# Loads of x on GpSimd's queue in a cross-attention kernel

## Chip, cores and metric

The kernel runs on one core of a Trainium2 chip. A time is the device time of one execution in microseconds (us), and the time before is the median of three executions. TensorE, VectorE, ScalarE, GpSimd and SyncE are the core's engines; in the profile they are PE (with PEld, its weight loads), DVE, ACT, POOL and SP.

## What is computed

The reference is a cross-attention over 32 batches of 512 rows of x, 640 wide, with 20 heads of 32, a context of 77 keys, an output projection with a bias, and the input x added at the end. The context holds only 77 tokens, so the slices for objects, others and images in the reference are empty and add nothing. In float32:

```python
residual = hidden_states
q = _heads(hidden_states @ to_q_w)
h_txt = _sdpa(q, _heads(ehs_txt @ to_k_w), _heads(ehs_txt @ to_v_w))
...
out = _merge(h_txt) + SCALE_OBJ * _merge(h_obj) + SCALE_OTH * _merge(h_oth) + SCALE_IP * _merge(h_ip)
out = out @ to_out_w + to_out_b
out = (out + residual) / RESCALE
```

## The kernel before

**Precision.** Each matrix product is done as three products of split numbers (a high part and a rest, `PAIRS`), so a projection of 640 channels takes 15 matmuls for 512 columns.

**Phases.** Up to about 285 us the kernel computes keys and values of all batches and stores them in device memory (`k_dram`, `v_dram`). After that runs a pipeline of N = 160 slots: slot n treats batch b = n // 5 and a group of four heads j = n % 5. `slot(n)` writes out the order of work of every engine by hand (`manual_schedule`): each engine, SyncE with its DMA issues too, does its instructions in program order, and waits at each for what it needs.

**A slot.** Per slot there are four score tiles of 128 rows (`scores`), the exponentials on ScalarE (`exps`), and the following work of other heads:

- `queries(n + 1, ...)`: the next slot's q, on TensorE (L332), and `split_q`, which splits it on ScalarE and VectorE (L343 to L349).
- `normalize(n - 1, ...)`: GpSimd multiplies the last slot's exponentials by the reciprocal sums (L400).
- `transpose_p(n - 1)`: VectorE transposes them into the tile `z` (L407), and four DMAs write z to device memory (`pd`, L414). z has one buffer, so the next transpose waits until these four have read it. `load_p` reads them back in the wanted order (`raw`, L423 and L424), some slots later.
- `cast_p`, `rest_p`, `last_p`: the split of the loaded p on ScalarE (L431, L437), VectorE (L438) and GpSimd (L445), into `pp`.
- `values`: TensorE multiplies pp and the values (L459), eight passes; the last two use the part that `last_p` writes.
- `piece`: TensorE's output projection (L489); `finish` adds it to a row block of the residual `xr` on VectorE (L517) and stores it (L521). `load_residual` loads that block (L478), and `add_bias` adds the bias to it on GpSimd (L482), before.
- `refill`: parts of the keys and values of this or the next batch (L309, L312, L319).

**x.** `load_x(b)` loads a whole batch of x into the tile `xs` with four DMAs of 320 KB, one for each 32 partitions; each consists of 32 x 16 runs of 160 floats. The tile has one buffer. `transpose_x` turns it in four pieces on VectorE (L272), one in slot 0, two in slot 1 and one in slot 2 of the batch ahead of its use; `split_x` splits it into `xt`, five blocks on ScalarE (L279) and GpSimd (L280), in slots 2 and 3. In slot 4 of batch b the tile is free and `load_x(b + 2)` fills it. The loads for batches 0 and 1 are issued ahead of the pipeline.

**Order in the middle of slot 4.** After the second score tile come `load_p`, `refill` (nothing in slot 4), `finish`, `load_x`, `load_residual`, and `add_bias`. GpSimd's work in a slot comes in the order `normalize`, `last_p`, `add_bias` and, in slots 2 and 3, `split_x`. All DMAs of the kernel are issued by SyncE.

Of the kernel before, what the change touches and what calls it, by code (L numbers as in the profile page):

```python
# [24 lines left out]
Q = 32  # L25
# [25 lines left out]
def kernel(  # L51
# [25 lines left out]
    nc = tc.nc  # L77
# [181 lines left out]

    xts, raws, pps, ats, xss, pds, sms, pqs, pas, xrs, pos = ({} for _ in range(11))  # L260

    def load_x(b):

        xs = main.tile([P, S // Q, C // 4], F32, tag="xs", name="xs")
        src = x[b].rearrange("(a j) (q u) -> q j a u", j=Q, q=4)
        for q in range(4):
            nc.sync.dma_start(xs[q * Q : (q + 1) * Q, :, :], src[q])
        xss[b] = xs

    def transpose_x(b, i):  # L270
# [82 lines left out]
    def scores(n, t):  # L353
        b, j = divmod(n, NC_)
        g = GROUP_OF[j]
        qt, (kb, kc) = qts[n % 2], kbs[g]
        jg = j - GROUPS[g][0]
        sc = ps.tile([P, S], F32, tag="sc", name="sc", bufs=3)
        half = KCOLS // 2
        for m, (cols, keys_) in enumerate(  # L360
            (
                (slice(0, KCOLS), kb[:, jg]),
                (slice(0, half), kc[:, jg, 0]),
                (slice(half, KCOLS), kc[:, jg, 1]),
            )
        ):
            nc.tensor.matmul(  # L367
                sc[:, cols],
                qt[:, m, t * P : (t + 1) * P],
                keys_,  # L370
                start=(m == 0),
                stop=(m == 2),
            )
        nm = main.tile([P, HPC], F32, tag="nm", name="nm", bufs=3)
        nc.vector.tensor_reduce(  # L375
            nm, sc[:, :KCOLS].rearrange("p (h k) -> p h k", k=NKEY), AX.X, ALU.max, negate=True
        )
        return sc, nm
# [14 lines left out]
    def sums(n):  # L393
        rs = main.tile([P, NQ * HPC], F32, tag="rs", name="rs", bufs=2)
        nc.vector.reciprocal(rs, sms.pop(n))  # L395
        return rs

    def normalize(n, rs):
        pf = pnb[n % 2][:, :, :NKEY]
        nc.gpsimd.tensor_tensor(  # L400
            pf, pf, rs.unsqueeze(2).to_broadcast([P, NQ * HPC, NKEY]), ALU.mult
        )
# [17 lines left out]
    def load_p(n):  # L420
        pd = pds.pop(n)
        raw = late[0].tile([P, 3, S], F32, tag="raw", name="raw", bufs=2)
        nc.sync.dma_start(raw[:, 0:2, :], pd[0 : 2 * P, :].rearrange("(k p) q -> p k q", p=P))  # L423
        nc.sync.dma_start(raw[:64, 2, :], pd[2 * P :, :])  # L424
        raws[n] = raw

    def cast_p(n):

        raw = raws[n]
        pp = late[0].tile([P, 5, S], FPR, tag="pp", name="pp", bufs=1)  # L430
        nc.scalar.copy(pp[:, 0:2, :], raw[:, 0:2, :])  # L431
        pps[n] = pp

    def rest_p(n):

        raw, pp = raws[n], pps[n]
        nc.scalar.copy(pp[:64, 4, :], raw[:64, 2, :])  # L437
        nc.vector.tensor_tensor(  # L438
            pp[:, 2:4, :], raw[:, 0:2, :], pp[:, 0:2, :].bitcast(F32), ALU.subtract
        )  # L440

    def last_p(n):

        raw, pp = raws.pop(n), pps[n]
        nc.gpsimd.tensor_tensor(  # L445
            pp[64:, 4, :], raw[:64, 2, :], pp[:64, 4, :].bitcast(F32), ALU.subtract
        )
# [27 lines left out]
    def load_residual(b, t, xr=None):  # L475
        if xr is None:
            xr = late[0].tile([P, C], F32, tag="xr", name="xr", bufs=3)
        nc.sync.dma_start(xr, x[b, t * P : (t + 1) * P, :])  # L478
        xrs[b, t] = xr
# [31 lines left out]
    def finish():  # L511

        while closed:
            b, t, h = closed.pop(0)
            xr = xrs[b, t]
            cols = slice(h * HALF, (h + 1) * HALF)
            nc.vector.tensor_tensor(  # L517
                xr[:, cols], pos.pop((b, t, h))[:, :HALF], xr[:, cols], ALU.add
            )
            if h == 1:  # L520
                nc.sync.dma_start(out[b, t * P : (t + 1) * P, :], xr)  # L521
# [11 lines left out]
    RESIDUAL = {1: (1, 0), 2: (1, 1), 3: (1, 2), 4: (1, 3)}  # L533
# [9 lines left out]
    def refill(b, j, part):  # L543

        heads = range(2 * part, 2 * part + 2)
        segments = SEGMENTS[4 * part : 4 * part + 4]
        if j == 0:
            load_keys(b, 1, heads)
        elif j == 1:
            load_values(b, 0, segments)  # L550
        elif j == 2 and b + 1 < B:
            load_keys(b + 1, 0, heads)
        elif j == 3:
            load_values(b, 1, segments)

    def slot(n, beside=None):
        b, j = divmod(n, NC_)
        ahead, more = n + 1 < N, b + 1 < B
        back, first = PIECES[j]
        bo_, has_out = b - back, b >= back  # L560
        xsplits = SPLIT_X.get(j, ((), ())) if more else ((), ())
        turns = TRANSPOSE_X.get(j, ((), (), ())) if more else ((), (), ())
        taken, second = takes.get(n), seconds.get(n)

        refill(b, j, 0)
        if taken is not None:
            cast_p(taken)
        s = scores(n, 0)
        if taken is not None:
            rest_p(taken)  # L570
        if n:
            normalize(n - 1, sums(n - 1))
        if taken is not None:
            last_p(taken)
        exps(n, 0, *s)
        if ahead:
            queries(n + 1, 0, 2)
        s = scores(n, 1)
        if n - LAG + 1 in pds and n > LATE:
            load_p(n - LAG + 1)  # L580
        refill(b, j, 1)
        finish()
        if j == 4 and b + 2 < B:
            load_x(b + 2)
        if j in RESIDUAL and b >= RESIDUAL[j][0]:
            load_residual(b - RESIDUAL[j][0], RESIDUAL[j][1])
        if j in BIAS and b >= BIAS[j][0]:
            add_bias(b - BIAS[j][0], BIAS[j][1])
        exps(n, 1, *s)
        for i in turns[0]:  # L590
            transpose_x(b + 1, i)
        if ahead:
            queries(n + 1, 2, NC_)
        s = scores(n, 2)
        if n:
            transpose_p(n - 1)
        if ahead:
            split_q(n + 1)
        exps(n, 2, *s)
        for c in xsplits[0]:  # L600
            split_x(b + 1, c)
        if has_out:
            piece(bo_, first)
        if taken is not None:
            values(taken)
        if beside:
            beside()
        s = scores(n, 3)
        finish()
        for i in turns[1]:  # L610
            transpose_x(b + 1, i)
        if taken is not None:
            split_a(taken)
        for c in xsplits[1]:
            split_x(b + 1, c)
        exps(n, 3, *s)
        if has_out:
            piece(bo_, first + 1)
        for i in turns[2]:
            transpose_x(b + 1, i)  # L620
        if second is not None:
            cast_p(second)
            rest_p(second)
            last_p(second)
            take(second)
            if second + 2 in pds and second + 2 not in takes.values():
                load_p(second + 2)
# [66 lines left out]

    with tc.manual_schedule(engines=ENGINES):
        g0, gn = GROUPS_KV[-1]
        load_x(0)
        load_keys(0, 0)
        for h in range(2):
            context_values(g0, gn, 0, h, psv)  # L700
        for i in range(NQ):
            transpose_x(0, i)
        for c in range(NC_):
            split_x(0, c, nc.gpsimd if c % 2 else nc.vector)
        load_x(1)
        for t0 in (P, 2 * P):
            for h in range(2):
                context_values(g0, gn, t0, h, psv)
        queries(0, 0, NC_)
        split_q(0)  # L710
        for n in range(LATE):
            slot(n, (lambda: context_values(g0, gn, 3 * P, n // 2, psv)) if n % 2 else None)
        psv.release()
        kvp.release()
        late.append(ctx.enter_context(tc.tile_pool(name="late", bufs=1, reuse_waits="tile")))
        late.append(
            ctx.enter_context(tc.tile_pool(name="psl", bufs=1, space=PSUM, reuse_waits="tile"))
        )
        load_p(0)
        load_p(1)  # L720
        wos.append(late[0].tile([P, NC_, 2, C], FPR, name="wo_s"))
        for n in range(LATE, LATE + 4):
            slot(n)
            for k in {LATE: (0, 1), LATE + 1: (2, 3), LATE + 2: (4,)}.get(n, ()):
                nc.sync.dma_start(wos[0][:, k].bitcast(F32), wo_dram[:, k].bitcast(F32))
        for n in range(LATE + 4, N):
            slot(n)
        end()
# [40 lines left out]
```

## Time and profile before

| What | Value |
|---|---|
| Median of 3 runs | 2026.93 us (2025.39 to 2027.08) |
| Profiled execution | 2018.67 us, span 2016.9 us |
| Mean granted TensorE clock | 0.989 |
| Busy, VectorE / ScalarE / GpSimd | 1354.7 / 1588.0 / 981.9 us |
| Loads of x: issues, time of one issue, issue to landing | 128, 0.487 us, 7.5 us (medians) |
| Writes of p: issues, time of one issue, issue to landing | 640, 0.520 us, 3.6 us (medians) |

The profile is of one execution, and all its times are from the start of the span. A row of a timeline has the start, the time taken, the engine, the line, the operation, what is written from what, and in brackets the idle time of the engine before it with what ended that. A row of waits reads: who waited for whom, microseconds in total, times, the longest.

### The profile page before, as it was taken

What the parts mean: (1) busy time and instruction counts of PE and PEld (TensorE: products, weight loads), DVE (VectorE), ACT (ScalarE), POOL (GpSimd) and SP (SyncE); (2) the same over time, 40 slices, a digit from 0 to 9 for tenths busy, and PEclk for the clock granted to TensorE, in tenths of its full rate; (3) what the DMA queues carried; (4) which work ended last, traced back from release to release, by engine and by line L of the source; (5) the groups of instructions that cost most, each with busy time, mean ns of one, the idle gap of its engine ahead of it and who ended that gap; (6) DMA issues with size and microseconds to landing.
All of it is one profiled execution on the core that took longest, in us unless ns stands there. A gap on an engine that the chain in (4) does not pass through costs nothing.

```text
span 2016.9 us, 38271 instructions
## 1 busy us (share of the span) xinstructions
PE 1963.4 (97%) x11012; PEld 1763.5 (87%) x11012; DVE 1354.7 (67%) x2159; ACT 1588.0 (79%) x6377; POOL 981.9 (49%) x617
## 2 busy tenths in 40 slices
PE   9999997899999999999999999999999999999998
PEld 7889986789888988888898888888888888988898
DVE  4443225777777777777777677777777777777764
ACT  3321128889889988888898899899898889989993
POOL 0000023555555555555556555666555655555554
PEclk9999998999999999999999999999999999999999
DMA  7993366888888888888988888888888888888875
GB/s 172 221 255 108 105 148 151 222 222 221 223 223 220 226 218 226 217 218 218 229 226 220 208 227 229 222 223 218 217 222 219 218 224 218 228 222 222 222 202 169
DMA packets 555997, 423.55 MB, mean 210 GB/s; under 512 B 170191, under 2 KB 459501, under 8 KB 555789
## 3 DMA queue, kind: packets, MB, share of 16 engines
q1 hardware_dynamic: 555789, 421.10, 82.4%
q8 instruction: 91, 1.49, 0.3%
q14 instruction: 117, 0.96, 0.1%
HBM read 245.61 MB, written 175.32 MB: 209 GB/s over the span
## 4 chain that ended last, share of the span: by engine, by line
PE 54%; DMA 19%; SPq 8%; POOL 6%; issue 5%; ACT 4%; DVE 4%; DVEq 0%; POOLq 0%; ACTq 0%
PE pq L332 17%; PE po L489 15%; DMA pd<-z 8%; PE pa L459 8%; PE sc L367 6%; POOL pn L400 4%; PE pv L197 4%; PE pk L168 4%; DMA xs<-in_x_dram 3%; DMA raw<-pd 3%; SPq L414 2%; DVE qt L349 2%; ACT pn L385 2%; POOL pp L445 2%; DMA kb<-k_dram 1%
## 5 line engine op out<-in xcount | busy, mean ns | idle before, releaser
L385 ACT ACTIVATE pn<-sc,nm 128x77 f32<-128x77 f32 x2560 | 799.2, 329 | 109.3 <-DVE nm L375 96.5
L400 POOL TENSOR_TENSOR pn<-pn,rs 128x1232 f32<-128x1232 f32 x160 | 364.5, 2278 | 692.6 <-DVE rs L395 541.2
L489 PE MATMUL po<-wo_s,at 128*128 128x320 f32 x3840 | 627.6, 313 | 1.4 <-DVE xr L517 1.4
L332 PE MATMUL pq<-xt,wq_s 128*128 128x512 f32 x2400 | 622.5, 400 | 0.0
L489 PEld LDWEIGHTS po<-wo_s,at 128*128 128x128 f32 x3840 | 567.0, 189 | 2.0 <-DVE xr L517 1.7
L385 ACT ACTIVATION_READ_ACCUMULATOR pn<-sc,nm 128x1 f32 x2560 | 530.6, 207 | 0.0
L332 PEld LDWEIGHTS pq<-xt,wq_s 128*128 128x128 f32 x2400 | 429.7, 190 | 77.5 <-POOL xt L280 0.2
L375 DVE TENSOR_REDUCE nm<-sc 128x4 f32<-128x308 f32 x640 | 294.0, 460 | 264.3 <-PE sc L367 258.1
L459 PE MATMUL pa<-pp,vb 128*128 128x512 f32 x1280 | 337.7, 402 | 19.6 <-ACT pp L431 9.9
L407 DVE STREAM_TRANSPOSE z<-pn 128x1280 f32<-128x1280 f32 x160 | 241.8, 1511 | 119.2 <-DMA pd<-z 62.4
L459 PEld LDWEIGHTS pa<-pp,vb 128*128 128x128 f32 x1280 | 242.5, 197 | 68.3 <-POOL pp L445 20.7
L367 PEld LDWEIGHTS sc<-kc,qt 128*128 128x128 f32 x1280 | 213.3, 189 | 40.9 <-issue 13.9
L367 PE MATMUL sc<-kc,qt 128*128 128x154 f32 x1280 | 227.1, 256 | 13.6 <-DVE qt L349 12.9
L438 DVE TENSOR_TENSOR pp<-raw,pp 128x1024 fp32r<-128x1024 f32 x160 | 196.2, 1226 | 50.1 <-ACT pp L431 34.3
L445 POOL TENSOR_TENSOR pp<-raw,pp 64x512 fp32r<-64x512 f32 x160 | 209.4, 1309 | 36.4 <-ACT pp L437 24.3
L349 DVE TENSOR_TENSOR qt<-pq,qt 64x512 fp32r<-64x512 f32 x320 | 214.3, 670 | 7.5 <-ACT qt L343 3.1
L280 POOL TENSOR_TENSOR xt<-xs,xt 128x512 fp32r<-128x512 f32 x157 | 199.7, 1299 | 16.8 <-ACT xt L279 12.2
L482 POOL TENSOR_TENSOR xr<-xr,bias 128x640 f32<-128x640 f32 x128 | 201.2, 1573 | 12.0 <-POOL pp L445 2.7
L347 ACT CAST qt<-qt 64x512 fp32r<-64x512 f32 x320 | 198.1, 619 | 9.0
L367 PE MATMUL sc<-kb,qt 128*128 128x308 f32 x640 | 196.0, 306 | 1.2 <-ACT qt L343 1.2
L431 ACT CAST pp<-raw 128x1024 fp32r<-128x1024 f32 x160 | 170.1, 1063 | 1.3 <-DVE at L105 0.8
L104 ACT CAST at<-pa 128x512 fp32r<-128x512 f32 x160 | 94.9, 593 | 75.5 <-PE pa L459 72.8
(41 smaller groups left out, 1536.3 us busy)
## 6 DMA issues: line engine op xcount, KB each, us to landing
pd<-z SPq DMA_DIRECT2D x640, 160.0 KB, 3.6
raw<-pd SPq DMA_DIRECT2D x160, 512.0 KB, 4.1
xs<-in_x_dram SPq DMA_DIRECT2D x128, 320.0 KB, 7.5
xr<-in_x_dram SPq DMA_DIRECT2D x128, 320.0 KB, 3.8
out_dram<-xr SPq DMA_DIRECT2D x128, 320.0 KB, 3.3
raw<-pd SPq DMA_DIRECT2D x160, 128.0 KB, 4.2
v_dram<-vs SPq DMA_DIRECT2D x19, 640.0 KB, 4.0
k_dram<-ks SPq DMA_DIRECT2D x80, 128.0 KB, 2.4
```

Of the source, the lines that this page charges most:

```text
L280: engine.tensor_tensor(parts[1], src, parts[0].bitcast(F32), ALU.subtract)
L332: nc.tensor.matmul(pqs[n], wq_s[:, k, a, j * P : (j + 1) * P], xts[b, k][:, c, :], start=(k == 0 and m == 0), stop=(k == NC_ - 1 and m == 2),)
L349: nc.vector.tensor_tensor(qt[r, 1 + w, :], pq[r], qt[r, 0, :].bitcast(F32), ALU.subtract)
L367: nc.tensor.matmul(sc[:, cols], qt[:, m, t * P : (t + 1) * P], keys_, start=(m == 0), stop=(m == 2),)
L375: nc.vector.tensor_reduce(nm, sc[:, :KCOLS].rearrange("p (h k) -> p h k", k=NKEY), AX.X, ALU.max, negate=True)
L385: nc.scalar.activation(pnb[n % 2][:, at, :NKEY], sc[:, i * NKEY : (i + 1) * NKEY], AF.Exp, bias=nm[:, i : i + 1], accum_out=sms[n][:, at : ...
L400: nc.gpsimd.tensor_tensor(pf, pf, rs.unsqueeze(2).to_broadcast([P, NQ * HPC, NKEY]), ALU.mult)
L407: nc.vector.transpose(z.rearrange("p b t j -> p t b j"), pn.rearrange("p (t h) k -> p t (h k)", t=NQ).rearrange("p t (b i) -> p t b i", i=Q),)
L445: nc.gpsimd.tensor_tensor(pp[64:, 4, :], raw[:64, 2, :], pp[:64, 4, :].bitcast(F32), ALU.subtract)
L459: nc.tensor.matmul(pas[n], vb[:, t, :, a], pp[:, c, :], start=(m == 0), stop=(m == len(PASSES) - 1),)
L482: nc.gpsimd.tensor_tensor(xrs[b, t], xrs[b, t], bias, ALU.add)
L489: nc.tensor.matmul(pos[b, t, h][:, :HALF], ats[b * NC_ + j][:, a, t * P : (t + 1) * P], wos[0][:, j, c, h * HALF : (h + 1) * HALF], start= ...
```

## The change

`load_x` takes the issuing engine as an argument, GpSimd if none is named. The two loads ahead of the pipeline stay on SyncE; those in slot 4, 30 of them with four DMAs each, are issued by GpSimd, at its place in program order between `last_p` and `add_bias` of that slot. In the program `load_residual` now stands ahead of `load_x`. Shapes, buffers and all arithmetic stay.

```diff
-    def load_x(b):
+    def load_x(b, engine=nc.gpsimd):
...
-            nc.sync.dma_start(xs[q * Q : (q + 1) * Q, :, :], src[q])
+            engine.dma_start(xs[q * Q : (q + 1) * Q, :, :], src[q])
...
+        if j in RESIDUAL and b >= RESIDUAL[j][0]:
+            load_residual(b - RESIDUAL[j][0], RESIDUAL[j][1])
         if j == 4 and b + 2 < B:
             load_x(b + 2)
-        if j in RESIDUAL and b >= RESIDUAL[j][0]:
-            load_residual(b - RESIDUAL[j][0], RESIDUAL[j][1])
...
-        load_x(0)
+        load_x(0, nc.sync)
...
-        load_x(1)
+        load_x(1, nc.sync)
```

## The prediction

> **What bounds the kernel now.** I read the page's engine shares first, then the waits of each engine over the steady stretch (380 to 1925 us), then the timelines of all engines over one batch.
>
> ```profile
> span 2016.9 us, 38271 instructions
> PE 1963.4 (97%) x11012; PEld 1763.5 (87%) x11012; DVE 1354.7 (67%) x2159; ACT 1588.0 (79%) x6377; POOL 981.9 (49%) x617
> ...
> q1 hardware_dynamic: 555789, 421.10, 82.4%
> ```
>
> TensorE sets the pace: 97% busy, granted clock 1.00 in the steady windows, and one slot after another starts its projection of queries at 962.26, 972.59 and 982.90 us, so a slot that nothing disturbs takes 10.32 us and a batch of five 51.6. All DMAs are in one hardware queue, and GpSimd issues none. What can still be won is what TensorE waits for. Its waits in the steady stretch, and VectorE's beside them:
>
> ```profile
> PE sc L367 <- DVE qt L349: 9.0, 24, 0.8
> PE pa L459 <- POOL pp L445: 6.4, 24, 0.8
> ...
> DVE z L407 <- DMA pd<-z: 62.4, 23, 4.0
> ```
>
> Both TensorE waits come about once per batch, as the wait of the transpose of p for the writes of the former p (z has one buffer) does. The timeline of VectorE shows where: a batch's first slot, right behind the load of x.
>
> ```profile
> 987.30 0.48 DVE L375 TENSOR_REDUCE nm<-sc 128x4 f32<-128x308 f32 x1 [1.78 <-PE sc L367]
> 990.59 1.51 DVE L407 STREAM_TRANSPOSE z<-pn 128x1280 f32<-128x1280 f32 x1 [2.81 <-DMA pd<-z]
> 992.02 1.37 DVE L349 TENSOR_TENSOR qt<-pq,qt 64x512 fp32r<-64x512 f32 x2
> 993.42 0.48 DVE L375 TENSOR_REDUCE nm<-sc 128x4 f32<-128x308 f32 x1
> ...
> 994.34 0.83 DVE L272 STREAM_TRANSPOSE xs<-xs 128x640 f32<-128x640 f32 x1
> ```
>
> And the timeline of SyncE shows why: four loads of x (4 x 320 KB) enter the queue ahead of the writes of p.
>
> ```profile
> 976.65 1.95 SPq L267 DMA_DIRECT2D xs<-in_x_dram  x4
> 978.64 1.21 SPq L478 DMA_DIRECT2D xr<-in_x_dram  x1
> 979.90 3.50 SPq L414 DMA_DIRECT2D pd<-z  x4
> ```
>
> Those four writes land 8.2 to 9.5 us after issue; the kernel's median for such a write is 3.6, and the four issued from 969.44 also took 3.6. The last lands when z is given free, at 990.5, while GpSimd had its normalized p ready at 987.61. The split of q starts late, TensorE waits 0.27 us for it, and a slot later 0.23 for GpSimd's pp, which the same delay pushed back. The whole price is read from the starts of the normalizations: from 420.41 to 1891.63 us, 28 batches took 52.54 us each. The steps into slots 2, 3, 4 and 0 are the same in all, about 9.53, 10.12, 10.50 and 9.98; only the step from slot 0 to slot 1 varies, between 11.38 and 14.24. Against 51.6 this is 0.94 us a batch, 28 us for the 30 batches that load an x this way. The waits that the view books make only 15.4; the rest lies in matmuls drawn longer than their spacing.
>
> **The change, part by part.**
> Removed from SyncE: 120 of the 128 loads of x, four in each of 30 batches, 4 x 0.487 = 1.95 us a batch. SyncE isn't the bound, and by itself this only lets the residual load and the writes of p go out earlier; the writes wait for the transpose, which ends at 979.17, so they gain some 0.7 us.
>
> The residual's load, now ahead in the program, is on another engine than the load of x, and its order against SyncE's other work is otherwise kept: nothing.
>
> Taken out of the queue ahead of p: 1.31 MB. The stretch from 979 to 984 us moves 200 GB/s and that from 982.6 to 993 moves 229, so 1.31 MB is 5.7 to 6.6 us of all engines; the writes of p are late by 8.9 - 3.6 = 5.3. If x goes beside them in a queue of its own, with half the engines' time at worst, 0.66 MB of p takes 6 us and is read out by about 986, before the 987.61 at which it is wanted. The wait of VectorE goes, and with it up to 28 us. On the same 16 engines the sum of the bytes stays, so x gives up what p gains, and x is what is late next. At half of 220 GB/s its 1.31 MB takes 11.9 us from about 980, so it lands near 992. It is wanted by the first transpose of x: 994.34 in this batch, about 991.5 without VectorE's 2.81 us stall. VectorE can be some 2.5 us late there before TensorE waits (that is 2.81 less the 0.27 that came through). So a wait of half a microsecond lies in that cover, and is costed at nothing; without cover it is 0.5 x 30 = 15 us.
>
> Added on GpSimd: four DMA issues per batch, between the pp of slot 4 and the bias add of that slot. Their own wait, for the readers of xs, is long over (the last split of x ends at 973.96). Queued behind them are the bias add (1.57 us; its rows are finished only in the next batch's first slot), then the normalization of slot 0, and behind that the pp of slot 0, for which TensorE's value matmuls wait.
>
> ```profile
> 977.71 1.29 POOL L445 TENSOR_TENSOR pp<-raw,pp 64x512 fp32r<-64x512 f32 x1
> 979.08 1.57 POOL L482 TENSOR_TENSOR xr<-xr,bias 128x640 f32<-128x640 f32 x1
> 985.33 2.28 POOL L400 TENSOR_TENSOR pn<-pn,rs 128x1232 f32<-128x1232 f32 x1 [4.68 <-DVE rs L395]
> 987.69 1.29 POOL L445 TENSOR_TENSOR pp<-raw,pp 64x512 fp32r<-64x512 f32 x1
> ```
>
> The hole of 4.68 us before that normalization stands in 28 of the 29 batches that I listed, at 4.66 to 4.71. Behind it there is a little more: the value matmuls run from 988.89 to 990.77, eight passes of 0.235; the last two need pp, at 990.30, and pp ends at 988.98, so 1.3 us. The cover is 6.0 us for four issues, 1.5 each. What is over it stops TensorE every batch: 30 us per microsecond.
>
> The trace has no DMA issued by GpSimd, so the issue is bounded. From below: SyncE's issue of the same load, 0.487 us, 1.95 for four. From above: the slowest issue in the trace, 2.67 us (a residual load on SyncE with the queue full), 10.7 for four. GpSimd's own nearest row is an instruction that steps through as many items as this load has pieces: a load is 32 x 16 = 512 runs of 640 bytes, and its 128x512 subtraction takes 1299 ns. I take that, 1.30: 5.2 us for four, inside the 6.0, so nothing reaches TensorE. At 2.67 it is 4.7 over, +141 us; at 0.487 nothing.
>
> The Trainium skill, in "DMA: Bandwidth & Descriptors" (Issuing engines are not separate DMA queues), speaks against the gain: all issuers' DMAs run on the same 16 engines, and issuing from several only saves the sequencer's time. By that sentence alone nothing would be won here and the time would be the old one. The same page (Queues, rings and completion order) has each engine take turns between the queues; by that the write of p no longer stands behind all of x. The rows of 8.9 against 3.6 us decide for me that standing in line is what costs. The same page (SWDGE vs HWDGE vs iDMA) says that software on GpSimd builds these descriptors, and gives about 1 us to the first byte; four of that as an estimate would be 4.0 us, inside the cover too.
>
> **The sum.** Gain bounds are 15.4 (booked waits) and 28 us (steps); I take 24, nearer the steps, since they measure the whole delay, less something for batches in which x comes late. GpSimd's issues, the x wait and SyncE's part: 0. The profiled execution took 2018.67 us (span 2016.9), so 2018.67 - 24 = 1994.7. The median of the runs shown, 2026.93, is 8.3 above that execution, and the result will be such a median: 2026.93 - 24 = 2003.
>
> **The rivals.**
> GpSimd becomes late (the other side): an issue costs more than 1.5 us plus the gain's worth. It decides from 4t = 6.0 + 24/30 = 6.8, t = 1.7. For it speaks that 512 runs per load are many, and that the step behind is on TensorE's path; against it, the 128x512 row. In the middle of 1.7 to 2.67, at 2.3: 9.2 - 6.0 = 3.2 us x 30 = 96, less 24, so 2099; at 2.67, 2144.
>
> x lands too late: if its queue gets a third of the engines, 1.31 MB at 73 GB/s takes 18 us, landing at 998, some 4 us behind the 994 from which TensorE pays: 120 - 24, so 2123; with 2 us, 2063. Against it: today VectorE never waits for x, not once in 116 transposes of the steady stretch.
>
> No effect: p waits as long beside x as behind it, since the engines' time is full there (the queue's packets take 97% in the slot from 982.6): 2027, with SyncE's issue time gaining nothing.
>
> Half and half: t between 1.5 and 1.7 eats the gain, 2003 to 2027.
>
> **How the numbers follow.** Forecast 0.47, own range 1996 to 2018 (28 us and 0.15% of run spread at the low end, 9 us of gain at the other). GpSimd late 0.35, x late 0.06, no effect 0.05, half and half 0.07. A change under 0.2%, 4 us, can't be told from none. Faster: 0.47 + 0.03 = 0.50; same 0.05 + 0.03 = 0.08; slower 0.35 + 0.06 + 0.01 = 0.42. The range leaves out the upper half of the late GpSimd (0.17): 1996 to 2099.
>
> **What would show it.** Right: a second DMA queue in the queue table; writes of p from slot 4 landing near 6 us; VectorE's 62 us wait for them gone; steps from slot 0 to 1 at 11.4; the hole before GpSimd's normalization shrunk but open. Wrong: that hole closed and the normalization ended by GpSimd's own issues, TensorE's wait for pp grown to over a microsecond a batch, or VectorE waiting for xs before its transpose.

## The result and the profile after

The changed kernel takes 2006.24 us (median of 4 runs, 2005.16 to 2008.14) against 2026.16 for the kernel before in the same comparison: a ratio of 0.9905, 95% interval 0.9888 to 0.9922, 19.9 us less. Repeated beside the experiments, it was 0.9874 (0.9853 to 0.9894). The two profiled executions differ by less, 2018.67 and 2006.13 us, so by 12.5: that of the kernel before was faster than any of its four runs (2023.31 to 2027.08).

The lines of the page after that answer to those of before (span, busy time by engine, DMA queues, GpSimd's issues):

```profile
span 2004.3 us, 38335 instructions
PE 1957.5 (98%) x11012; PEld 1761.6 (88%) x11012; DVE 1355.5 (68%) x2159; ACT 1593.0 (79%) x6377; POOL 1058.5 (53%) x737
...
q1 hardware_dynamic: 492429, 381.77, 71.6%
q0 software_dynamic: 11520, 39.33, 8.0%
...
xs<-in_x_dram POOLq DMA_DIRECT2D x120, 320.0 KB, 7.1
```

x has its own queue, and there 39.33 MB go in 11,520 packets, 3.4 KB each on average; before, every run of 640 bytes was a packet. The long packets cost the engines less: the queues' packets took 82.4% of 2016.9 us before and 71.6 + 8.0 = 79.6% of 2004.3 us now, which is 2.2 us of all engines less in each of 30 batches. The busy sum of GpSimd has grown by 76.6 us, about what 120 issues at 0.652 us each (median) make. The waits of the steady stretch (380 to 1925 us) in the changed kernel:

```profile
PE pa L459 <- POOL pp L445: 3.9, 17, 0.3
PE sc L367 <- DVE qt L349: 3.1, 9, 0.4
...
DVE z L407 <- DMA kc<-k_dram: 32.0, 12, 3.4
DVE z L407 <- DMA pd<-z: 30.7, 15, 2.8
```

TensorE's waits have halved, from 15.4 to 7.0 us. VectorE's for z have fallen by a fifth only, from 77.1 to 62.7 us: the transposes still wait 30.7 us for writes of p and 32.0 more under the name of the kc load (a load of keys), beside 62.4 and 14.7 before. The timeline of one batch shows that both names stand for one thing. SyncE's issues, to begin with:

```profile
972.48 0.54 SPq L478 DMA_DIRECT2D xr<-in_x_dram  x1
973.51 2.89 SPq L414 DMA_DIRECT2D pd<-z  x4
976.50 0.87 SPq L521 DMA_DIRECT2D out_dram<-xr  x1
```

The writes of p go out 0.03 us after their transpose has ended. GpSimd's timeline beside it, with x between pp and the bias add, and a hole of 2.14 us left before the normalization (4.68 before):

```profile
973.26 2.61 POOL L267 DMA_DIRECT2D xs<-in_x_dram  x4
975.92 1.57 POOL L482 TENSOR_TENSOR xr<-xr,bias 128x640 f32<-128x640 f32 x1
979.64 2.27 POOL L400 TENSOR_TENSOR pn<-pn,rs 128x1232 f32<-128x1232 f32 x1 [2.14 <-DVE rs L395]
```

And VectorE's next transpose into z:

```profile
985.36 1.51 DVE L407 STREAM_TRANSPOSE z<-pn 128x1280 f32<-128x1280 f32 x1 [3.29 <-DMA kc<-k_dram]
```

Of the four writes of p issued from 973.51, the first two land at 979.27 and 980.86, the last two at 984.93 and 985.24; x lands at 984.74. The transpose of z starts 0.12 us behind the last write. So the writes still wait for x, only not all of them.

In the mean over 23 batches (the last slots from about 660 to 1817 us), counted in us from the start of the normalization in the last slot:

| | before | changed |
|---|---|---|
| issue of x, first to end of last | 1.06 to 3.29 | 3.60 to 6.20 |
| issue of p's four writes | 5.12 to 8.72 | 3.85 to 6.46 |
| writes of p land, first and last | 13.53, 15.04 | 8.16, 14.67 |
| x landed | 12.10 | 14.16 |
| next transpose of z starts | 15.22 | 14.82 |
| normalization of slot 1 starts | 22.44 | 22.01 |

The step that varied, slot 0 to slot 1, is 0.4 us shorter (12.46 and 12.07); 30 of them are 12 us, the difference of the two profiled executions. The other 7 us between the medians stand in no trace.

SyncE's own rows show what held its writes of p before. The residual's load, issued right behind x, took 1.74 us to issue in the mean of these batches, and it takes 0.53 in the change; the writes of p took 0.86 each and take 0.62. There is a second brake in these kernels, which the trace's semaphores show: SyncE's loads and writes report their landing on eight semaphores in turn, and of the 2573 issues before none starts until the one eight earlier has landed (230 start within 0.1 us of it). So a slow load can hold up issues that have nothing to do with it.

### The profile page after: what moved, and what is told of

Its sections match the earlier page's. It is cut to its first block, busy times and chain, and to the rows that moved or that the text cites. A ratio compares the mean times of both kernels' runs of the same rounds, so it can differ in the third digit from the quotient of the medians.

```text
span 2004.3 us, 38335 instructions
## 1 busy us (share of the span) xinstructions
PE 1957.5 (98%) x11012; PEld 1761.6 (88%) x11012; DVE 1355.5 (68%) x2159; ACT 1593.0 (79%) x6377; POOL 1058.5 (53%) x737
## 3 DMA queue, kind: packets, MB, share of 16 engines
q1 hardware_dynamic: 492429, 381.77, 71.6%
q0 software_dynamic: 11520, 39.33, 8.0%
q8 instruction: 91, 1.49, 0.3%
## 4 chain that ended last, share of the span: by engine, by line
PE 70%; DMA 5%; POOL 5%; ACT 5%; issue 4%; DVE 3%; SPq 2%; DVEq 0%; POOLq 0%; ACTq 0%
PE pq L332 22%; PE po L489 21%; PE pa L459 11%; PE sc L367 8%; PE pk L168 4%; PE pv L197 4%; POOL pn L400 3%; DMA pd<-z 3%; ACT pn L385 2%; DMA kc<-k_dram 2%; POOL pp L445 2%; DVE qt L349 1%; ACT pp L431 1%; DVE z L407 1%; DMA raw<-pd 1%
```

## Experiments

All ratios are against the kernel before, run on the same chip in the same comparison. There were three comparisons, on three chips (medians of 2033 to 2036 us for the kernel before): the first four experiments, then the halves on GpSimd and on SyncE behind p with no x and the change again, then the halves ahead of p, SyncE held and the work on GpSimd. "Last write" and "loads of p" are means from the traces, in the count of the table above.

**The order alone.**

```diff
-        if j == 4 and b + 2 < B:
-            load_x(b + 2)
         if j in RESIDUAL and b >= RESIDUAL[j][0]:
             load_residual(b - RESIDUAL[j][0], RESIDUAL[j][1])
+        if j == 4 and b + 2 < B:
+            load_x(b + 2)
```

> The order of the two loads alone: the residual's load goes ahead of the load of x on SyncE, which still issues both. Theory A (the writes of p stand behind x in one queue, and a queue of its own for x is what the change brings) and theory B (what counts is that GpSimd's x goes in packets of 4480 bytes in place of 640 and so takes less of the engines' time): no difference, within 5 us of the kernel before, writes of p in the last slot still landing after 8 to 10 us. Theory C (SyncE's order and issue time are what the change brings): a part of the gain, 5 us or more.

1.0000 (0.9978 to 1.0023). Last write at 15.28. Theory C's share for the order is nil. SyncE's first write went out at 4.42, but its last only by 9.91: behind x in the same queue the four issues took 5.5 us in all, where in other slots they take 2.6.

**SyncE, with x behind p.** `load_x(b + 2)` stays on SyncE and moves behind `transpose_p(n - 1)`.

> The loads of x stay on SyncE, in the same slot, but are issued behind the four writes of p. Theories A and B: the writes of p land in about 3.6 us in that slot, VectorE's waits for them (62 us in the steady stretch before, 63 after, if those booked to kc are counted there) fall under 15, and the time falls by 15 to 28 us, 1998 to 2011, as much as with GpSimd or more. Theory C: SyncE issues as much as before, so no gain, 2026. Against a gain: x lands some 4 us later, and the keys stand behind it; then VectorE waits for xs before its first transpose.

1.0042 (1.0024 to 1.0061): no gain, as only theory C had it, but for a reason that none gave. The writes of p land at 9.40 and VectorE's wait for them falls from 62.4 to 4.6 us. TensorE's one wait in this kernel's steady stretch:

```profile
PE pa L459 <- POOL pp L445: 37.5, 30, 2.5
```

And SyncE's largest sum of waits for x there, at the second load of p:

```profile
SPq L424 <- DMA xs<-in_x_dram: 38.9, 29, 2.4
```

What stands behind x now is the load of the same p in the next slot: the issues eight earlier are loads of x, and in all 23 batches the second part of p's load starts within 0.1 us of the landing of one of them. The load lands at 20.72 (19.81 before), and pp comes late once in each of 30 batches. The price had moved from the write of p to its load.

**x on ScalarE's queue.** The change with `engine=nc.scalar` as the default.

> The loads of x at the place of the change, but issued by ScalarE: a second queue whose packets are 640 bytes, like before. Theory A: like the change, 2000 to 2011, less what four issues of about 0.5 us cost ScalarE. Theory B: packets of nearly equal size share the engines more evenly, so the writes of p land in 6 to 7 us against 8.6 in the change, and VectorE's waits for them fall under 30 us; but x takes the engines as long as before, and the drain isn't shorter: the gain is 10 us at most.

0.9926 (0.9897 to 0.9954), some 15 us. Theory B's evener sharing isn't there. ScalarE reached its issues earlier, at -1.29, so x now met the load of p of the last slot, and from 978 to 984 us the two queues (q10 has x, q1 all that SyncE issues) got this:

```profile
q10 hardware_dynamic: 1726, 1.07, 95.8%
q1 hardware_dynamic: 114, 0.23, 18.0%
```

The load of p landed at 9.18 in place of 4.84; the step from slot 4 to slot 0 grew from 9.98 to 11.43, and that from slot 0 to 1 shrank from 12.46 to 10.59. The last write landed at 13.96, 10.0 us from the first issue, because SyncE was held at the issues, as its timeline shows in one batch:

```profile
978.95 0.57 SPq L478 DMA_DIRECT2D xr<-in_x_dram  x1
981.27 8.04 SPq L414 DMA_DIRECT2D pd<-z  x4
```

Four issues that take 2.5 us elsewhere took 8.04 here and 7.4 in the mean. The second to fourth waited for what was issued eight earlier, the two loads of p and the residual's, which x had made late: in 67 of 69 cases they start within 0.1 us of that landing. So it was SyncE's own late loads that held it, not ScalarE's queue as such.

**x in long runs.** The kernel before, with

```diff
-            nc.sync.dma_start(xs[q * Q : (q + 1) * Q, :, :], src[q])
+            nc.sync.dma_start(part.rearrange("p a u -> p (a u)"), rows[q])
```

where `rows[q]` are 128 consecutive rows of x, four to a partition.

> The kernel before, with the loads of x from the third batch on taking the same bytes in runs of 10,240 bytes (consecutive rows to a partition), so x comes to other places of the tile and what is computed from it is not the reference's; all shapes, counts and orders stay. Theory A: x still stands ahead of p in the one queue, the writes of p land after 7 us or more and the gain is under 8 us. Theory B: x drains in about 1.31 MB at 330 to 400 GB/s = 3.3 to 4 us, the writes of p land within 6 us, and the gain is 15 us or more.

0.9886 (0.9859 to 0.9914), some 23 us: theory A's "under 8 us" falls, and theory B's "15 us or more" came. But B's way to it isn't there: the last write lands at 14.38, 8.8 to 11.3 us from first issue, so there is neither a drain of 4 us nor p within 6. What this kernel has in common with the change is that SyncE is done with p's writes sooner, 3.95 to 7.04 against 5.12 to 8.72, because its issues behind x are short again; in one batch:

```profile
973.60 0.43 SPq L483 DMA_DIRECT2D xr<-in_x_dram  x1
974.07 3.18 SPq L419 DMA_DIRECT2D pd<-z  x4
```

So long packets alone, in the one queue, win what the change wins. Whether they do it through SyncE's shorter issues or through the engines' time that they save isn't separated by this run.

So a theory D took the place of A to C: the engines are full in this stretch, and what counts is how much stands ahead of p, in whichever queue, when p's writes and loads get issued.

**x in two halves, on GpSimd.**

```diff
-            load_x(b + 2)
+            load_x(b + 2, a1=S // Q // 2)
+        if j == 0 and 2 <= b + 1 < B:
+            load_x(b + 1, a0=S // Q // 2)
```

> The change, with each load of x cut in two along the rows: four issues of 160 KB by GpSimd in the last slot, four in the next slot, behind the pp of that slot. The last write of p in the last slot landed 15.04 us after that slot's normalization began in the kernel before and 14.67 in the change, so x in a second queue doesn't stand aside for p. Theory D (the engines are full in this stretch, and what counts is the bytes ahead of p, in whichever queue): 0.66 MB less at 220 GB/s is 3 us, the last write lands near 11.7, before the normalized p is ready at 12.35, VectorE's wait goes, and the time falls by 10 to 16 us more than in the change, a ratio of 0.982 to 0.986. Theory A (a queue of its own is what counts, its size not): like the change, 0.990, or worse by the issues. Against both: the second half holds up the load of p in the first slot.

0.9800 (0.9778 to 0.9821), 1991.77 us. The last write lands at 11.73, as worked out, and the next transpose starts at 12.57. Theory A, for which the queue and not the amount mattered, falls. The ratio is below theory D's range, and so are those of the next kernel and of no x at all below theirs: between medians the price is larger than in the traces.

**The same halves on SyncE, behind p.**

> The same halves on SyncE, each behind the four writes of p of its slot, with no GpSimd. Theory D: p's writes go first, and the loads of p in the next slot have 0.66 MB less before them than with the whole x behind p, where they landed at 20.72 against 19.81 before; so they land 2 to 3 us sooner, and the time is 0.983 to 0.992 of before, near that of the halves on GpSimd. Theory A: without a queue of its own x delays either the writes or the loads of p, 1.000 or above.

0.9796 (0.9775 to 0.9817), 1993.14 us: without GpSimd and without a second queue, as fast. The waits of TensorE and of VectorE in the steady stretch:

```profile
PE po L490 <- DVE xr L518: 1.1, 1, 1.1
PE pa L460 <- POOL pp L446: 0.3, 1, 0.3
...
DVE z L408 <- DMA pd<-z: 8.2, 7, 2.7
```

The last write lands at 9.13, the loads of p in the next slot at 17.08, and a batch takes 51.61 us.

**The halves on SyncE, ahead of p,** at the place of the kernel before:

> The kernel before with only the cut of x in halves: four loads of 160 KB ahead of the writes of p in the last slot, the other four in the next, all on SyncE and at the place of the kernel before. Theory D (bytes ahead of p, whatever the queue): in the last slot 0.66 MB less are ahead, 3 us, so the last write lands near 12.0 and VectorE's wait goes there, but in the first slot the other half is ahead of the writes of that slot, which have more time: 0.980 to 0.987. If it is the place behind p that made the halves on SyncE as fast as no x at all: 0.990 or above.

0.9855 (0.9830 to 0.9880). The last write lands at 12.70, not 12.0, and z still waits, but now a little in every slot (0.5 to 1.3 us), of which TensorE feels little: 2.3 us for pp, 2.0 for the residual, and no group of waits for the split of q. So the cut alone gives some 0.7 of what there is (1.45% here, 2.04% on the other chip with the place behind p), and the place behind p the rest.

**No x at all.**

> The kernel before with the loads of x from the third batch on left out; the tile keeps what it holds, and all other work stays. It gives the whole price of these loads. All theories: VectorE's wait for the writes of p goes, batches take 51.5 to 51.7 us in place of 52.55, so the ratio is 0.983 to 0.986 (28 to 33 us). If it is much lower, TensorE's waits weren't all of the price.

0.9804 (0.9783 to 0.9825). A batch takes 51.61 us, and TensorE waits 0.3 us for pp in the whole steady stretch. This is the price of these loads in the kernel before, and the halves, on GpSimd or behind p on SyncE, win all of it within the intervals (in the traces a batch takes 51.85 us with the halves on GpSimd).

**The change again.**

> The change as it is, on this chip beside the others: 0.990 again if the gain doesn't hang on the chip, within 0.988 to 0.993.

0.9874 (0.9853 to 0.9894): a little more gain here than in the first comparison and just outside the range given, with intervals that overlap; the last write at 14.62, as in the first (14.67).

**SyncE held, x on GpSimd.** The change with seven small loads on SyncE in front:

```diff
+            for q in (0, 1, 2, 3, 0, 1, 2):
+                nc.sync.dma_start(held[q * Q : (q + 1) * Q, :], x[b, q * Q : (q + 1) * Q, :64])
             load_x(b + 2)
```

> The change with seven small loads (8 KB each, into a tile that nobody reads) on SyncE behind the residual's load of the last slot, so that SyncE is held and the writes of p start at about 5.1 us behind that slot's normalization, as in the kernel before, in place of 3.85; x stays on GpSimd's queue. Theory D, its part on the change (it wins because p's writes start sooner, the first two of them land ahead of x, and the rest end a little sooner): the gain falls away, 0.996 to 1.002. Theory A (the second queue): the gain stays, 0.987 to 0.992.

1.0045 (1.0022 to 1.0068). SyncE was held longer than meant: p's writes went out from 7.87 to 10.16, not from 5.1. They then land from 14.33 on, at 15.54 the last, behind x (13.66) although x is in another queue. VectorE's waits in this kernel:

```profile
DVE z L408 <- DMA pd<-z: 91.0, 29, 4.9
```

So a queue of its own for x, long packets included, brings nothing if p's writes come late. What the 1.3 us of the change are worth by themselves isn't measured by this, since the hold was 4.0 us. Taken in proportion, as an estimate, 1.3 of the 4.0 are 0.28 of the 0.87 us by which the last write landed later (15.54 against 14.67), and the change had won 0.37.

**More work on GpSimd.** Behind the four issues, `nc.gpsimd.tensor_tensor(extra, bias[:, :256], bias[:, :256], ALU.add)` three and six times:

> The change with three more adds of 128x256 on GpSimd behind the four loads of x, into a tile that nobody reads. One load took GpSimd 0.652 us, four 2.6, against the 5.2 of the prediction, so of the cover of 6.0 us before TensorE has to wait 3.4 are left. An add of 128x256 is an estimate of 1.0 us from 128x512 (1.30) and 128x1232 (2.28): 3.0 in all, inside the cover. If the cover is as predicted: like the change, 0.985 to 0.992 of before. If it is only the open hole before the normalization (2.1 us): 0.9 us over in 30 batches, 27 us more, 1.000 or above.

0.9884 (0.9857 to 0.9910): like the change. The adds took 0.61 us each, 1.8 in all, so they fit even into the hole of 2.1 us, and this run doesn't decide between the two covers. Yet the normalization of slot 0 ends 1.2 us later, at 13.42, with 1.39 us of the hole still open behind the bias add, because VectorE was late with what it waits for (from the timelines of both engines in one batch):

```profile
668.77 1.99 POOL L589 TENSOR_TENSOR extra<-bias 128x256 f32<-128x256 f32 x3
670.72 1.56 POOL L483 TENSOR_TENSOR xr<-xr,bias 128x640 f32<-128x640 f32 x1
670.97 2.40 DVE L439 TENSOR_TENSOR pp<-raw,pp 128x1024 fp32r<-128x1024 f32 x1 [0.21 <-ACT pp L432]
673.68 2.27 POOL L401 TENSOR_TENSOR pn<-pn,rs 128x1232 f32<-128x1232 f32 x1 [1.39 <-DVE rs L396]
```

VectorE's split of p (L439) takes 2.35 us in the mean while GpSimd's bias add runs beside it, and 1.23 in the change, where the bias add is over by then. Even so TensorE waited only 4.0 us for pp in the steady stretch (3.9 in the change): a normalization 1.2 us late is inside the cover.

> The same with six adds: 6.0 us against the 3.4 that are left, 2.6 over in 30 batches, 78 us above the change, a ratio of 1.02 to 1.03, with TensorE's waits for GpSimd's pp grown to over 1.5 us a batch. If TensorE's lateness from the writes of p, 2.4 us on VectorE in the change, covers it too, then under 30 us, 1.00.

1.0018 (1.0002 to 1.0035), less than forecast because the adds were shorter, 0.756 us each. GpSimd's extra work is then 2.6 + 4.5 = 7.1 us, 1.1 more than the cover of 6.0, and the hole is gone. TensorE's waits in this kernel:

```profile
PE pa L460 <- POOL pp L446: 36.1, 30, 1.8
```

36.1 us in 30 batches are 1.2 each, about what is over the cover, where a cover of the hole alone (4.7 us) would leave 2.4. The rival "GpSimd late" had the right mechanism, and its point, a gain lost at 6.8 us, is about right.

## Why the prediction was right, and where it wasn't

**The bound and the price held.** TensorE sets the pace, and the loads of x cost 0.94 us a batch: without them a batch took 51.61 us, where the prediction had read 51.6 from undisturbed slots. The whole price was in reach, 28 us by the profile; between medians it is more, 40 us (0.9804 of 2035.5), on a chip where the kernel before is slower too. Of this price the change won less than half by the traces (12.5 of 28 us) and some 0.65 between medians of one chip (1.26% of 1.96%); the prediction had 24 of 28.

**The step that failed is "if x goes beside them in a queue of its own ... 0.66 MB of p takes 6 us and is read out by about 986".** It assumed that a second queue gets half the engines' time at worst. In the changed kernel the writes of the last slot took 10.8 us (median, first issue to last landing), no less than before (10.0), and VectorE's waits stayed. Of the five signs that the prediction named for being right, two came, the second queue and the hole still open; p's writes near 6 us, VectorE's wait gone and a step of 11.4 (12.07 was measured) did not. The DMA view of 978 to 982 us in the change shows that the assumption was bad (packets, MB, share of the engines):

```profile
q0 software_dynamic: 222, 0.78, 73.7%
q1 hardware_dynamic: 589, 0.29, 33.4%
```

In these 4 us GpSimd's queue moves 0.78 MB in 222 packets of 3.5 KB, SyncE's 0.29 in 589 of 0.5 KB. The Trainium skill has each engine take turns between the queues packet by packet ("DMA: Bandwidth & Descriptors", Queues, rings and completion order). The packets of these views don't show such turns: 222 against 589 here, and 1726 against 114 with x on ScalarE's queue, where x's packets were the shorter ones and x still got most of the bytes. Whether the page means the packets of these views no run here shows, and how the engines divide their time stays open; in both views the queue with x has most of it. The halves on SyncE show that no second queue is needed.

**What was costed at "some 0.7 us" and set aside is what the gain seems to hang on.** The 0.7 was one batch's delay of the first write, and the last was not looked at. SyncE, freed of x, starts p's writes 1.27 us sooner and is done with them 2.26 us sooner, so two of the four land well ahead of x. The kernels with a whole x issued in the last slot, ahead of p's writes or beside them (means of 23 batches, in us from the start of the normalization; the batch is that of the one traced execution):

| | SyncE's issue of p ends | last write of p lands | VectorE's wait for z in slot 0 | batch | ratio |
|---|---|---|---|---|---|
| long runs | 7.04 | 14.38 | 2.12 | 52.11 | 0.9886 |
| the change | 6.46 | 14.67 | 2.43 | 52.22 | 0.9905, 0.9874 |
| before | 8.72 | 15.04 | 2.79 | 52.59 | 1 |
| order alone | 9.91 | 15.28 | 3.05 | 53.00 | 1.0000 |
| SyncE held | 10.16 | 15.54 | 3.24 | 53.20 | 1.0045 |
| x on ScalarE | 11.21 | 13.96 | 1.49 | 52.59 | 0.9926 |

In the first five the batch goes with VectorE's wait, about one for one, and the wait with the landing of the last write. That is shown. That the landing goes with SyncE's issue is an ordering over these five, of which only SyncE held was made to test it, and x on ScalarE stands outside: its writes were issued last, though they landed first, and its batch paid at the load of p instead. A rival is open: in the change and with long runs x also takes the engines less time, 2.2 us a batch in the change, and no run has SyncE free with a whole x in short packets ahead of p. With SyncE held, the long packets alone won nothing. The sentence of the skill's page that the prediction argued down, that issuing from several engines only saves the sequencer's time (Issuing engines are not separate DMA queues), described this change better than the prediction did; the page calls that time usually small, and here it isn't negligible.

**The term of the gain was 24 us, measured 19.9 between the medians and 12.5 between the traces.** That the sum stood is luck. "The wait goes" was wrong: in slot 0 it fell only from 2.79 to 2.43 us on average. What helped is that a short wait costs TensorE nothing and only its excess is felt, so the excess goes first: in the table 0.36 us less wait is 0.37 us less batch, while without any wait a batch takes 51.61, which by an estimate from the table is reached already at a wait of some 1.6 us. The rest was made up by the kernel before, whose runs were slower than its traced execution.

**GpSimd's issue was sized at 1.30 us and is 0.652**, for a load of 512 runs; the row of SyncE's issue (0.487), taken as the lower bound, was nearer than the arithmetic row of 512 elements. As both lie under 1.5, it made no difference. The upper bound of 2.67 wasn't the slowest issue of the trace either: a weight load at 97.9 us took 2.88. The estimate from the Trainium skill, 4.0 us for four issues, took the 1 us to the first byte ("DMA: Bandwidth & Descriptors", Specifications) for time that GpSimd is held; it is held 2.6.

**x came in time**, at 14.16 behind the normalization, where the prediction had 16.6 (992 in the batch that it used), and 4.2 us (median) ahead of its first transpose; VectorE waits for x nowhere in the steady stretch. The rival "x lands too late" had no case.

**"No effect"** was nearer than its 0.05: its reason, that p waits as long beside x as behind it, is what the trace shows for the last two writes.

## What to carry to other kernels

Where one queue's burst holds up a short chain of small transfers, look at how many bytes are ahead of the chain in all queues together, and cut or move the burst: two halves in two slots, behind the chain and with no second queue, won 1.6 times what the change did on the same chip (2.04% against 1.26%). Ask which transfer will be next in line behind the moved one: with x behind the writes of p, the loads of p paid. And count the issue time of the engine that issues everything, even if it looks idle, and how many of its transfers may be on their way at once: what it issues later may be what the next wait hangs on.

## What was not expected of the hardware

- GpSimd's issue hardly depends on the runs in these two sizes: 0.660 us on average for 512 runs, 0.593 for the halves of 256 runs.
- Software-queued loads travel in long packets: each load of 512 runs of 640 bytes became 80 packets of 4480 or 2560 bytes, where SyncE's and ScalarE's had 512 of 640 bytes. For the same 39.33 MB the engines spent 8.0% of the span on GpSimd's queue and 10.1% on ScalarE's.
- SyncE never has more than eight loads and writes on their way in the kernel before, by their eight semaphores: of 2573 issues none starts ahead of the landing of the one eight earlier. Such waits made four issues take 7.4 us in place of 2.5 with x on ScalarE's queue.
- An elementwise instruction of VectorE took 2.35 us in place of 1.23 while GpSimd's bias add ran beside it (with three more adds).
- Runs of 10,240 bytes in place of 640 hardly made the burst drain sooner: x had landed 10.1 us from its first issue (median), in place of 10.9.
